# Gated cross-attention, one core: block transposes on VectorE in the setup, mp's rows placed by DMA, and the order of W1's loads

## Chip, cores and metric

The kernel runs on one core of a Trainium2 chip. The metric is device time of one execution in microseconds (us); lower is better. Everything is float32.

## What is computed

```python
memory_proj = einsum('bme,de->bmd', memory, W_mem)                 # mp
scores = einsum('bnd,bmd->bnm', x, memory_proj) / sqrt(D)
memory_context = einsum('bnm,bmd->bnd', softmax(scores), memory_proj)
gate = sigmoid(concat([x, memory_context], -1) @ W_gate.T + b_gate)
out = rmsnorm(x + gate * memory_context) * norm_w
```

There are 8 batches of 1024 rows of x (D = 1024), and for each batch 64 memory rows of 512 elements. W_gate has 1024 x 2048 elements. Its first half, here W1 (transposed), meets x. Its second half, W2, meets the memory context; since that context is a weighted sum of mp's rows, the kernel computes `mp @ W2 + b_gate` once, in the setup, and lets the attention weights sum its rows.

## The kernel before

**Setup.** All 512 memory rows (8 x 64, `BM`) are handled together, as 4 blocks of 128 rows (`NPAIR`).

1. Loads on SP's queue (`load`, L95-96) in this order: mem (4 transfers, L116-117), W_mem transposed as `wm` (4, L119-121), the bias, W2's first column half (16, L138), W1 into the tiles `ws1`, `ws7`, `ws3`, `ws2` (8 for each quarter, L143-148). W1 and W2 come in pieces of 32 partitions and 128 KB.
2. memT: 16 TensorE transposes into PSUM and 8 VectorE copies (L161-174). Four VectorE copies reorder wm into `wmp` (L176-184).
3. `pm`: 8 groups of 4 matmuls (the trace records two for each, so 64 in all) give mp transposed, chunk by chunk (L195-204). ScalarE and VectorE copy them in turn to the tiles `mpT`. After each second chunk ACT's queue stores the pair to `mpd` in HBM (`scratch`, L98-99).
4. mp's rows: 32 TensorE transposes of mpT into PSUM, 8 ScalarE copies, and 8 stores on ACT's queue to `mgd` (L206-221).
5. `pg`: 8 groups (n = 0 to 7, column half h by row block q) of 8 matmuls, again two records each, multiply mp by W2 (L400-425). VectorE adds the bias (`g2`, called g0 to g7 below by n), ACT stores it to `mgd` in two transfers. After group 0 the program issues the loads of W2's second half (`load_w2(1)`), of the first x tiles and of norm_w. After groups 0 to 5 VectorE gets its share of `w1_tasks`, the sums and differences of W1's quarters that the main loop multiplies by; after group 6 it gets `first`, the transposes and sums of the first x tiles.

**Main loop.** For each of 16 blocks of 512 rows, seven block products by a fast matrix multiplication scheme in two levels (`outer_product`, L533). Each has products kA, kB, kC, kD, kA, kE, kF in this order; VectorE and GpSimd combine them. x is transposed by VectorE in 32x32 blocks (`transpose_x`). The accumulators use five PSUM banks in rotation, the same that pm and pg use: kC of the very first product needs the bank that g7 still has to empty.

**What sets the order.** `pin` keeps the instructions of each engine in the order of the program. The framework puts the transfers of SP and ACT into an order of its own making and adds the waits between them. `gpool` has 7 buffers for W2 tiles, 4 for each half, so the fourth tile of the second half waits until group 3 has read the first tile of the first half. `mpT` takes the buffers of mem and of others, and the `mp` stages take wm's buffers (`xqpool`, 4), which the first x tiles take next.

```python
def inner_sums(o):
    w = ws[o]
    for s, a, b in ((T1, R12, R11), (T2, R22, T1), (R12, R22, R12), (T4, R21, T2)):
w1_tasks = [outer_sum(5, 7, 1), *inner_sums(1), outer_sum(6, 3, 5), outer_sum(7, 3, 7),
            outer_sum(4, 2, 6)] + [inner_sums of 6, 7, 5, 4, 2, 3]     # lambdas left out
```

Of the kernel before, what the change touches and what calls it, by code (L numbers as in the profile page):

```python
# [8 lines left out]
F32 = mybir.dt.float32  # L9
# [6 lines left out]
P = 128  # L16
# [4 lines left out]
def tile_gated_cross_attention_rmsnorm(  # L21
# [40 lines left out]
    nc = tc.nc  # L62
    B, N, D = x.shape
    M, E = mem.shape[1:]
# [3 lines left out]
    BM = B * M  # L68
    KD = D // P
    KE = E // P  # L70
    H = 512
    C = 256
    NPAIR = BM // P
    SCALE = 1.0 / float(D) ** 0.5
    Q4 = D // 4
# [3 lines left out]
    xqpool = ctx.enter_context(tc.tile_pool(name="xqpool", bufs=4))  # L79
    apool = ctx.enter_context(tc.tile_pool(name="apool", bufs=1))  # L80
    rot = ctx.enter_context(tc.tile_pool(name="rot", bufs=2))
# [3 lines left out]
    dram = ctx.enter_context(tc.tile_pool(name="dram", bufs=1, space=DRAM))  # L85

    pin = tc.keep_in_program_order

    def mm(o, lhsT, rhs, start, stop):
        pin(nc.tensor.matmul(o, lhsT, rhs, start=start, stop=stop, skip_group_check=True))  # L90

    def tt(eng, o, a, b, op):
        pin(eng.tensor_tensor(o, a, b, op))  # L93

    def load(o, i):  # L95
        pin(nc.sync.dma_start(o, i))

    def scratch(o, i):  # L98
        pin(nc.scalar.dma_start(o, i))

    def t4k(pool, shape, tag, name):
        return pool.tile(shape, F32, tag=tag, name=name)
# [7 lines left out]
    def bank(n, shape, name):  # L110
        return ps.tile(shape, F32, tag=banks[n % 5], name=name)


    memr = mem.rearrange("b m e -> (b m) e").rearrange("(q p) e -> p q e", p=P)
    mem_sb = [t4k(rot, [P, 2, E], "l2", f"mem_sb{i}") for i in range(2)]
    for q in range(NPAIR):  # L116
        load(mem_sb[q // 2][:, q % 2, :], memr[:, q, :])
    wm = []
    for k in range(KE):  # L119
        t = t4k(xqpool, [P, D], "xq", f"wm{k}")  # L120
        load(t, w_mem_t[k * P : (k + 1) * P, :])
        wm.append(t)
    bias_sb = t4k(small, [P, D], "junk", "bias_sb")
    load(bias_sb, b_gate.partition_broadcast(P))
    w2r = rows_by_chunk(w_gate_t[D:, :])
# [2 lines left out]
    def load_w2(h):  # L128
        for k in range(KD // 2):
            t = t4k(gpool, [P, 2, H], "gate", f"w2_{k}_{h}")  # L130
            for i in range(4):
                load(
                    t[32 * i : 32 * (i + 1), :, :],
                    w2r[i][:, 2 * k : 2 * k + 2, h * H : (h + 1) * H],
                )
            w2[k, h] = t
# [3 lines left out]
    w1r = rows_by_chunk(w_gate_t[:D, :])  # L140
    ws = {o: const.tile([P, 7, 2, C], F32, name=f"ws{o}") for o in range(1, 8)}
    R11, R21, R12, R22, T4, T1, T2 = range(7)
    for o, k, h in ((1, 0, 0), (7, 0, 1), (3, 1, 1), (2, 1, 0)):  # L143
        for i in range(4):
            for n in range(2):
                load(
                    ws[o][32 * i : 32 * (i + 1), 2 * n : 2 * n + 2, :, :],
                    w1r[i][:, 4 * k : 4 * k + 4, h * H + n * C : h * H + (n + 1) * C],
                )
    nw_sb = const.tile([P, D], F32, name="nw_sb")  # L150

    ident = const.tile([P, P], F32, name="ident")
# [3 lines left out]


    mpd = dram.tile([P, KD, BM], F32, name="mpd")
    mgd = dram.tile([B, 2, M, D], F32, name="mgd")
    memT = [t4k(apool, [P, 2, BM], f"a1{i + 1}", f"memT{i}") for i in range(2)]  # L160
    for q in range(NPAIR):  # L161
        pt = bank(q, [P, KE, P], f"pt_mem{q}")
        for k in range(KE):
            pin(
                nc.tensor.transpose(
                    pt[:, k, :], mem_sb[q // 2][:, q % 2, k * P : (k + 1) * P], ident
                )
            )
        for i in range(2):
            pin(  # L170
                nc.vector.tensor_copy(
                    memT[i][:, :, q * P : (q + 1) * P], pt[:, 2 * i : 2 * i + 2, :]
                )
            )
    wmp = []
    for k, tag in enumerate(("a21", "a22", "s1", "s2")):  # L176
        t = t4k(apool, [P, KD, P], tag, f"wmp{k}")
# [8 lines left out]
    mpT = [  # L186
        t4k(rot, [P, 2, BM], tag, f"mpT_{tag}_{i}")
        for tag in ("l2", "u")
        for i in range(2)
    ]  # L190

    def mp_rows(j, q):
        return mpT[j // 2][:, j % 2, q * P : (q + 1) * P]

    for j in range(KD):  # L195
        pm = bank(j, [P, BM], f"pm{j}")
        for k in range(KE):
            mm(pm, wmp[k][:, j, :], memT[k // 2][:, k % 2, :], k == 0, k == KE - 1)
        dst = mpT[j // 2][:, j % 2, :]
        if j % 2 == 0:  # L200
            pin(nc.scalar.copy(dst, pm))
        else:
            pin(nc.vector.tensor_copy(dst, pm))
            scratch(mpd[:, j - 1 : j + 1, :], mpT[j // 2])

    for q in range(NPAIR):  # L206
        stage = t4k(xqpool, [P, D], "xq", f"mp{q}")
        for h in range(2):
            pt = bank(2 * q + h, [P, 4, P], f"pt_mp{q}_{h}")
            for j in range(4):  # L210
                pin(nc.tensor.transpose(pt[:, j, :], mp_rows(4 * h + j, q), ident))
            pin(
                nc.scalar.copy(
                    stage.rearrange("p (i j r) -> p j i r", i=4, r=32)[
                        :, 4 * h : 4 * h + 4, :, :
                    ],
                    pt.rearrange("p j (i r) -> p j i r", r=32),
                )
            )
        for i in range(2):  # L220
            scratch(mgd[2 * q + i, 0], stage[i * M : (i + 1) * M, :])


    def outer_sum(o, a, b):
        tt(nc.vector, ws[o][:, 0:4, :, :], ws[a][:, 0:4, :, :], ws[b][:, 0:4, :, :], ALU.subtract)
# [4 lines that stand above are left out]
            yield lambda s=s, a=a, b=b: tt(  # L230
                nc.vector, w[:, s, :, :], w[:, a, :, :], w[:, b, :, :], ALU.subtract
            )
# [4 lines left out]
        *inner_sums(1),  # L237
        lambda: outer_sum(6, 3, 5),
        lambda: outer_sum(7, 3, 7),
        lambda: outer_sum(4, 2, 6),  # L240
    ] + [f for o in (6, 7, 5, 4, 2, 3) for f in inner_sums(o)]


    xq, A, S, L2, O = {}, {}, {}, {}, {}
    sTs, attns, attnTs, scs, mps, mgs = {}, {}, {}, {}, {}, {}
# [5 lines left out]
    def load_xq(q, t):  # L251
        b, n0 = where(q, t)
        xq[q, t] = tl = t4k(xqpool, [P, 4, Q4], "xq", f"xq{q}_{t}")
        src = x[b, n0 : n0 + P, :].rearrange("(s c) (i e) -> i c s e", c=32, i=4)
        for i in range(4):
            load(tl[32 * i : 32 * (i + 1), :, :], src[i])
# [47 lines left out]
    def inner_s(q, o, part):  # L304
        l11, l12, l21, l22 = quarters(left(q, o))
        if part == 0:
            L2[q, o] = t4k(rot, [P, 4, 2, P], "l2", f"l2_{q}_{o}")
        s1, s2, s3, s4 = (L2[q, o][:, i, :, :] for i in range(4))
        if part == 0:
            tt(nc.gpsimd, s1, l21, l22, ALU.add)  # L310
            tt(nc.gpsimd, s2, s1, l11, ALU.subtract)
        else:
            tt(nc.gpsimd, s3, l11, l21, ALU.subtract)
            tt(nc.gpsimd, s4, l12, s2, ALU.subtract)
# [71 lines left out]

    def load_mg(b):
        mgs[b] = t4k(small, [P, D], "mg", f"mg{b}")
        load(mgs[b], mgd[b].rearrange("g m d -> (g m) d"))


    first = [
# [7 lines left out]
    for h in range(2):  # L400
        cols = slice(h * H, (h + 1) * H)
        for q in range(NPAIR):
            pg = bank(n, [P, H], f"pg2_{h}_{q}")
            for k in range(KD):
                mm(pg, mp_rows(k, q), w2[k // 2, h][:, k % 2, :], k == 0, k == KD - 1)
            pool, tag = ((apool, "s4"), (small, "attnT"))[n % 2]
            stage = t4k(pool, [P, H], tag, f"g2_{h}_{q}")
            tt(nc.vector, stage, pg, bias_sb[:, cols], ALU.add)
            for i in range(2):
                scratch(mgd[2 * q + i, 1][:, cols], stage[i * M : (i + 1) * M, :])  # L410
            if n == 0:
                load_w2(1)
                for t in (0, 1, 2, 3):
                    load_xq(0, t)
                load(nw_sb, norm_w.partition_broadcast(P))
            if n < 6:
                while done < len(w1_tasks) * (n + 1) // 6:
                    w1_tasks[done]()
                    done += 1
            elif n == 6:  # L420
                for f in first:
                    f()
                for part in range(2):
                    inner_s(0, 1, part)
            n += 1
    load_mp(0)
    load_mg(0)


# [13 lines left out]
    def plan(q):  # L443
# [28 lines left out]
        if (q + 1) % QPB == 0:  # L472
            at(t0 + 10, load_mp, (q + 1) // QPB)
            at(t0 + 49, load_mg, (q + 1) // QPB)
# [219 lines left out]
```

## Time and profile before

| | |
|---|---|
| three runs | 1018.0, 1021.86, 1022.25 us; median 1021.86 us |
| the profiled execution | 1022.17 us, span 1020.4 us, mean granted TensorE clock 0.986 |
| TensorE / VectorE / ScalarE / GpSimd busy | 982.8 / 752.8 / 320.2 / 690.5 us |
| memT's transposes begin / pm begins | 3.32 / 9.03 us |
| transposes of mpT begin / pg begins | 39.59 / 46.71 us |
| first main product begins / its kC | 110.66 / 113.31 us |
| VectorE transpose of 128x512 (L267) | 693 ns mean |

Times inside the profile count from the start of the span. A row of the timeline tells start, duration, engine, line, operation, the tiles as out<-in, sizes, a count and, in brackets, how long the engine had been idle and what ended that. "SPq" and "ACTq" are the sequencers that issue transfers. In the tile names L93 and L90 are helper lines (`tt`, `mm`), so groups are told apart by tiles: ws and w are W1 and W2, g the stage of a pg group with its bias, l and s the sums made of x. A table by stages lists the stretch, its length, busy time and count for PE, PEld, DVE, ACT and POOL, and then granted clock, DMA share and GB/s. The chain of waits goes through the execution in order of time: start, duration, and what the end of the program was waiting for then.

### The profile page before, as it was taken

The page shows a single profiled execution, that of the slowest core. Times are in us where ns is not written, and L with a number is a line of the kernel's source. Part 1 is how long each engine was busy: PE and PEld are TensorE (multiplying, and loading weights), DVE is VectorE, ACT ScalarE, POOL GpSimd, SP SyncE. Part 2 cuts the span into 40 slices and gives each one's busy share as a digit, 9 for nine tenths or more (in the row PEclk, how much of TensorE's full clock was granted, in tenths as well). Part 3 has the DMA queues.
Part 4 walks back from the last instruction along what each step waited for, and adds up shares of the span by engine and source line. Part 5 has one row for each costly group of instructions (what it writes and reads, how often), then busy time and mean ns, then how long its engine had stood idle before and what let it go on. Part 6 is the DMA issues. An engine that isn't in the chain of part 4 may idle for free.

```text
span 1020.4 us, 14598 instructions
## 1 busy us (share of the span) xinstructions
PE 982.8 (96%) x4976; PEld 767.9 (75%) x4976; DVE 752.8 (74%) x1464; ACT 320.2 (31%) x587; POOL 690.5 (68%) x855
## 2 busy tenths in 40 slices
PE   7898999999999999999999999999999999999991
PEld 4443687888888887888788888888888878878881
DVE  2065667878878787878787787878787878878763
ACT  0200023334241523333243425142333334341512
POOL 0000477877878787878788787878787878878671
PEclk9899999999999999999999999999999999999996
DMA  7675608164643727192825455372718271543324
GB/s 246 185 187 152 169 1 171 68 140 108 153 106 83 186 76 162 63 187 83 166 73 132 117 131 128 81 188 69 170 62 184 86 165 70 125 128 83 84 72 134
DMA packets 75945, 126.78 MB, mean 124 GB/s; under 512 B 16224, under 2 KB 53088, under 8 KB 75872
## 3 DMA queue, kind: packets, MB, share of 16 engines
q1 hardware_dynamic: 64160, 86.01, 29.0%
q0 software_dynamic: 9216, 33.56, 17.9%
q10 hardware_dynamic: 2496, 6.29, 2.1%
q8 instruction: 39, 0.64, 0.3%
q14 instruction: 34, 0.28, 0.1%
HBM read 85.98 MB, written 39.85 MB: 123 GB/s over the span
## 4 chain that ended last, share of the span: by engine, by line
PE 82%; DVE 12%; DMA 3%; issue 1%; SPq 1%; ACT 0%; ACTq 0%; DVEq 0%; POOL 0%
PE kA L90 17%; PE pc L90 12%; PE kE L90 10%; PE kD L90 8%; PE kF L90 8%; PE kB L90 8%; PE kC L90 7%; PE psT L90 6%; DVE gate L518 5%; PE pm L90 3%; PE pg L90 3%; DVE gate L93 2%; DVE e L93 2%; DVE u L93 1%; DMA gate<-in_x 1%
## 5 line engine op out<-in xcount | busy, mean ns | idle before, releaser
L93 POOL TENSOR_TENSOR gate<-gate,u 128x256 f32<-128x256 f32 x336 | 269.1, 830 | 116.1 <-DVE u L93 92.8
L93 POOL TENSOR_TENSOR l<-a 128x256 f32<-128x256 f32 x128 | 125.5, 980 | 168.3 <-DVE a L267 104.8
L489 ACT ACTIVATE gate<-gate 128x512 f32<-128x512 f32 x128 | 79.3, 630 | 412.1 <-DVE gate L93 412.1
L90 PE MATMUL kA<-ws,a 128*128 128x256 f32 x512 | 131.5, 379 | 0.0
L90 PE MATMUL pc<-mg,attnT 64*128 64x256 f32 x512 | 127.4, 389 | 0.0
L518 DVE SCALAR_TENSOR_TENSOR gate<-gate,ss,nw_sb 128x512 f32<-128x512 f32 x128 | 121.6, 963 | 1.1
L90 PE MATMUL kC<-ws,l 128*128 128x256 f32 x448 | 115.1, 379 | 0.8 <-DVE g L93 0.8
L90 PE MATMUL kD<-ws,l 128*128 128x256 f32 x448 | 115.0, 379 | 0.0
L90 PE MATMUL kB<-ws,l 128*128 128x256 f32 x448 | 115.0, 379 | 0.0
L90 PE MATMUL kF<-ws,l 128*128 128x256 f32 x448 | 115.0, 379 | 0.0
L90 PEld LDWEIGHTS pc<-mg,attnT 64*128 64x128 f32 x512 | 90.6, 186 | 29.8 <-issue 21.2
L90 PEld LDWEIGHTS kA<-ws,a 128*128 128x128 f32 x512 | 97.2, 190 | 13.8 <-DVE s L93 0.2
L90 PE MATMUL kA<-ws,s 128*128 128x256 f32 x384 | 100.2, 383 | 0.0
L90 PEld LDWEIGHTS kB<-ws,l 128*128 128x128 f32 x448 | 85.1, 190 | 11.6
L90 PEld LDWEIGHTS kF<-ws,l 128*128 128x128 f32 x448 | 85.1, 190 | 11.6
L90 PEld LDWEIGHTS kC<-ws,l 128*128 128x128 f32 x448 | 83.8, 190 | 11.8 <-POOL l L93 1.1
L90 PEld LDWEIGHTS kD<-ws,l 128*128 128x128 f32 x448 | 83.9, 190 | 10.7
L93 DVE TENSOR_TENSOR gate<-gate,pc 128x512 f32<-128x512 f32 x128 | 87.1, 681 | 5.3 <-ACT gate L489 5.1
L267 DVE STREAM_TRANSPOSE a<-xq 128x512 f32<-128x512 f32 x128 | 86.0, 693 | 0.0
L93 POOL TENSOR_TENSOR l<-s 128x256 f32<-128x256 f32 x96 | 77.6, 809 | 8.4 <-PE kF L90 5.8
L90 PEld LDWEIGHTS kA<-ws,s 128*128 128x128 f32 x384 | 71.6, 190 | 15.2 <-DVE a L93 6.2
L93 DVE TENSOR_TENSOR u<-u,kB 128x256 f32<-128x256 f32 x112 | 46.8, 418 | 46.3 <-PE kB L90 41.6
(84 smaller groups left out, 1688.0 us busy)
## 6 DMA issues: line engine op xcount, KB each, us to landing
xq<-in_x SPq DMA_DIRECT2D x256, 128.0 KB, 5.5
gate<-in_x POOLq DMA_DIRECT2D x64, 512.0 KB, 7.4
out<-gate SPq DMA_DIRECT2D x64, 512.0 KB, 2.6
w<-in_w_gate_t SPq DMA_DIRECT2D x32, 128.0 KB, 3.3
ws<-in_w_gate_t SPq DMA_DIRECT2D x32, 128.0 KB, 2.9
mg<-mgd SPq DMA_DIRECT2D x8, 512.0 KB, 3.6
wm<-in_w_mem_t SPq DMA_DIRECT2D x4, 512.0 KB, 6.8
mgd<-mp ACTq DMA_DIRECT2D x8, 256.0 KB, 4.4
```

The source lines that it names most:

```text
L90: pin(nc.tensor.matmul(o, lhsT, rhs, start=start, stop=stop, skip_group_check=True))
L93: pin(eng.tensor_tensor(o, a, b, op))
L267: nc.vector.transpose(A[key][:, :, r * P : (r + 1) * P].rearrange("p j (s c) -> p s j c", c=32), xq[q, t].rearrange("p s (j r) -> p s j r" ...
L489: pin(nc.scalar.activation(g, g, AF.Sigmoid))
L518: nc.vector.scalar_tensor_tensor(g[:, cols], g[:, cols], rstd[:, t % 2 : t % 2 + 1], nw_sb[:, cols], ALU.mult, ALU.mult,)
```

## The change

The mem rows are loaded in 8 transfers of 32 partitions, in a layout from which four VectorE transposes in 32x32 blocks make memT without PSUM. For that wm's rows are loaded in another order, in 16 transfers of 32 partitions. mp's rows are made the same way: after each pair of pm chunks VectorE transposes four blocks of mpT into `mpq`, and after the last pair ACT issues 16 stores that put each 32-partition part in its place in `mgd`. The layout of `mgd` changes, so that a bias result is one store instead of two, and the load of mg is two instead of one. The last quarter of W1 (`ws2`) is loaded after W2's second half, and `outer_sum(4, 2, 6)`, which needs it, stands later in `w1_tasks`.

```diff
+    memq = [t4k(rot, [P, BM // 64, E // 4], "l2", f"memq{i}") for i in range(2)]
+    memr = mem.rearrange("b m e -> (b m) e").rearrange(
+        "(g s c) (i e) -> g i c s e", g=2, c=32, i=4
+    )
+    wm = [t4k(xqpool, [P, D], "xq", f"wm{k}") for k in range(KE)]
+    wmr = w_mem_t.rearrange("(i j r) d -> i j r d", i=4, r=32)
+    for g in range(2):
+        for i in range(4):
+            load(memq[g][32 * i : 32 * (i + 1), :, :], memr[g, i])
     for k in range(KE):
-        t = t4k(xqpool, [P, D], "xq", f"wm{k}")
-        load(t, w_mem_t[k * P : (k + 1) * P, :])
-        wm.append(t)
+        for i in range(4):
+            load(wm[k][32 * i : 32 * (i + 1), :], wmr[i, k])
...
-    for o, k, h in ((1, 0, 0), (7, 0, 1), (3, 1, 1), (2, 1, 0)):
+    def load_w1(o, k, h):
         for i in range(4):
             for n in range(2):
                 load(ws[o][...], w1r[i][...])
+    load_w1(1, 0, 0)
+    load_w1(7, 0, 1)
+    load_w1(3, 1, 1)
...
-    mgd = dram.tile([B, 2, M, D], F32, name="mgd")
+    mgd = dram.tile([2, BM, D], F32, name="mgd")
...
-    (16 TensorE transposes and 8 VectorE copies)
+    for g in range(2):
         for i in range(2):
             pin(
+                nc.vector.transpose(
+                    memT[i][:, :, g * (BM // 2) : (g + 1) * (BM // 2)].rearrange(
+                        "p j (s c) -> p s j c", c=32
+                    ),
+                    memq[g].rearrange("p s (j r) -> p s j r", r=32)[:, :, 2 * i : 2 * i + 2, :],
                 )
             )
...
+    mpq = [t4k(xqpool, [P, 4, Q4], "xq", f"mpq{g}") for g in range(4)]
     for j in range(KD):
...
+            pin(nc.vector.tensor_copy(src[:, 1, :], pm))
+            scratch(mpd[:, j - 1 : j + 1, :], src)
+            for g in range(4):
+                pin(
+                    nc.vector.transpose(
+                        mpq[g].rearrange("p s (j r) -> p s j r", r=32)[:, :, j - 1 : j + 1, :],
+                        src[:, :, g * P : (g + 1) * P].rearrange("p j (s c) -> p s j c", c=32),
+                    )
                 )
-    (32 TensorE transposes, 8 ScalarE copies, 8 stores to mgd)
+    for g in range(4):
+        for i in range(4):
+            scratch(
+                mgd[0, g * P : (g + 1) * P, i * Q4 : (i + 1) * Q4].rearrange(
+                    "(s c) e -> c s e", c=32
+                ),
+                mpq[g][32 * i : 32 * (i + 1), :, :],
+            )
...
         lambda: outer_sum(7, 3, 7),
+        *(f for o in (7, 5) for f in inner_sums(o)),
         lambda: outer_sum(4, 2, 6),
-    ] + [f for o in (6, 7, 5, 4, 2, 3) for f in inner_sums(o)]
+        *(f for o in (6, 4, 2, 3) for f in inner_sums(o)),
...
         mgs[b] = t4k(small, [P, D], "mg", f"mg{b}")
-        load(mgs[b], mgd[b].rearrange("g m d -> (g m) d"))
+        for g in range(2):
+            load(mgs[b][g * M : (g + 1) * M, :], mgd[g, b * M : (b + 1) * M, :])
...
-            for i in range(2):
-                scratch(mgd[2 * q + i, 1][:, cols], stage[i * M : (i + 1) * M, :])
+            scratch(mgd[1, q * P : (q + 1) * P, cols], stage)
             if n == 0:
                 load_w2(1)
+                load_w1(2, 1, 0)
                 for t in (0, 1, 2, 3):
                     load_xq(0, t)
```

More of the change, by code (lines that the diff above doesn't have):

```diff
@@ L111, in bank @@
         return ps.tile(shape, F32, tag=banks[n % 5], name=name)
[L114 to L118, printed above, removed]
+    memq = [t4k(rot, [P, BM // 64, E // 4], "l2", f"memq{i}") for i in range(2)]
[7 more added lines that the diff above has]
+            load(memq[g][32 * i : 32 * (i + 1), :, :], memr[g, i])
     for k in range(KE):
-        t = t4k(xqpool, [P, D], "xq", f"wm{k}")
-        load(t, w_mem_t[k * P : (k + 1) * P, :])
-        wm.append(t)
+        for i in range(4):
+            load(wm[k][32 * i : 32 * (i + 1), :], wmr[i, k])
     bias_sb = t4k(small, [P, D], "junk", "bias_sb")
@@ L158, in tile_gated_cross_attention_rmsnorm @@
     mpd = dram.tile([P, KD, BM], F32, name="mpd")
-    mgd = dram.tile([B, 2, M, D], F32, name="mgd")
+    mgd = dram.tile([2, BM, D], F32, name="mgd")
     memT = [t4k(apool, [P, 2, BM], f"a1{i + 1}", f"memT{i}") for i in range(2)]
[L161 to L168, printed above, removed]
+    for g in range(2):
         for i in range(2):
             pin(
-                nc.vector.tensor_copy(
-                    memT[i][:, :, q * P : (q + 1) * P], pt[:, 2 * i : 2 * i + 2, :]
+                nc.vector.transpose(
[3 more added lines that the diff above has]
+                    memq[g].rearrange("p s (j r) -> p s j r", r=32)[:, :, 2 * i : 2 * i + 2, :],
                 )
@@ L198, in tile_gated_cross_attention_rmsnorm @@
             mm(pm, wmp[k][:, j, :], memT[k // 2][:, k % 2, :], k == 0, k == KE - 1)
-        dst = mpT[j // 2][:, j % 2, :]
+        src = mpT[j // 2]
         if j % 2 == 0:
-            pin(nc.scalar.copy(dst, pm))
+            pin(nc.scalar.copy(src[:, 0, :], pm))
         else:
[L203 to L217, printed above, removed]
-                )
-            )
-        for i in range(2):
-            scratch(mgd[2 * q + i, 0], stage[i * M : (i + 1) * M, :])
+            pin(nc.vector.tensor_copy(src[:, 1, :], pm))
[6 more added lines that the diff above has]
+                    )
+                )
+    for g in range(4):
[5 more added lines that the diff above has]
+                mpq[g][32 * i : 32 * (i + 1), :, :],
+            )
     def outer_sum(o, a, b):
@@ L239, in tile_gated_cross_attention_rmsnorm @@
         lambda: outer_sum(7, 3, 7),
+        *(f for o in (7, 5) for f in inner_sums(o)),
         lambda: outer_sum(4, 2, 6),
-    ] + [f for o in (6, 7, 5, 4, 2, 3) for f in inner_sums(o)]
+        *(f for o in (6, 4, 2, 3) for f in inner_sums(o)),
+    ]
     xq, A, S, L2, O = {}, {}, {}, {}, {}
@@ L408, in tile_gated_cross_attention_rmsnorm @@
             tt(nc.vector, stage, pg, bias_sb[:, cols], ALU.add)
-            for i in range(2):
-                scratch(mgd[2 * q + i, 1][:, cols], stage[i * M : (i + 1) * M, :])
+            scratch(mgd[1, q * P : (q + 1) * P, cols], stage)
             if n == 0:
                 load_w2(1)
+                load_w1(2, 1, 0)
                 for t in (0, 1, 2, 3):
```

## The prediction

> **What bounds the kernel now.** I read the page's busy shares first, then the table by stages, then the chain of waits in the first 110 us, then the rows of SP and VectorE in it.
>
> ```profile
> PE 982.8 (96%) x4976; PEld 767.9 (75%) x4976; DVE 752.8 (74%) x1464; ACT 320.2 (31%) x587; POOL 690.5 (68%) x855
> ```
> TensorE bounds the whole, and its idle time lies at the start. By stages (PE busy first, granted clock third from last):
>
> ```profile
> 9.00:39.60 30.60, 30.57 (x65) 13.27 (x66) 4.16 (x6) 2.34 (x4) 0.00 (x0) 1.00 0.65 198
> 39.60:46.71 7.11, 4.08 (x33) 3.37 (x32) 0.69 (x1) 3.23 (x6) 0.00 (x0) 0.94 0.68 195
> 77.21:89.93 12.72, 8.94 (x17) 3.32 (x16) 6.06 (x10) 0.00 (x0) 0.00 (x0) 0.88 0.76 197
> 400.00:600.00 200.00, 199.15 (x1064) 163.37 (x1064) 162.90 (x326) 70.69 (x129) 157.49 (x195) 1.00 0.44 114
> ```
> The main loop has no slack to give; the change doesn't touch it. What it can move is when that loop starts: its third product, kC, at 113.31 us. The chain of waits shows what leads there:
>
> ```profile
> 9.03 30.73 PE pm L90 x64
> ...
> 64.40 2.28 DMA mgd<-g
> 66.68 0.02 issue
> 66.70 0.31 SPq L96
> ...
> 68.48 3.10 DMA ws<-in_w_gate_t
> ...
> 80.24 2.66 DMA mgd<-g
> 82.90 0.02 issue
> 82.92 0.31 SPq L96
> ```
> A load of W1 on SP starts when a store of ACT has landed, though the two share no data. The rows of SP fit one rule: SP's and ACT's transfers stand in one common order, and each waits for the landing of the one eight places ahead (the fourth piece of W2 starts at 8.19, when the first wm, eight ahead, has landed). In all, to 115 us:
>
> ```profile
> SPq L96 <- DMA mgd<-g: 29.2, 8, 5.1
> SPq L96 <- DMA mpd<-mpT_u: 10.2, 1, 10.2
> SPq L96 <- DMA mpd<-mpT_l: 9.7, 2, 5.1
> ```
> So weights arrive at the pace of TensorE's own results, and late weights stop TensorE and VectorE:
>
> ```profile
> 82.28 1.98 PE L90 MATMUL pg<-w,mpT_u 128*128 128x512 f32 x4 [1.47 <-DMA w<-in_w_gate_t]
> 86.58 3.56 PE L90 MATMUL pg<-w,mpT_u 128*128 128x512 f32 x4 [2.31 <-DMA w<-in_w_gate_t]
> 113.31 1.10 PE L90 MATMUL kC<-ws,l 128*128 128x256 f32 x4 [0.75 <-DVE g L93]
> ```
>
> **The skill.** "DMA: Bandwidth & Descriptors", Rules for kernel authors, says that transfers to separate partition parts serialize and that one of 128 partitions should be used. The trace agrees in part: four wm of 512 KB land 1.27 us apart (8.17 to 11.98), while 128 KB pieces of 32 partitions land 0.57 to 0.60 us apart, 2.3 us for 512 KB. "TensorE: Matmul & The Clock Gate", Part 1, says that TensorE runs at half speed after idling until it has been busy some 3.4 us. Here matmuls come every 0.85 us until 15.1 and every 0.43 us after, and again 0.85 from 46.71 to 52.8. "VectorE: DVE Perf Modes", The three transpose paths, says that VectorE transposes within 32x32 blocks only; the kernel's own x transposes do so in 0.69 us per 128x512.
>
> **Step 1, loads of mem and wm: later by 4.3 us.** Eight transfers become 24 of 128 KB. The first should land at 3.2 (issue at 0.74, plus the 2.5 us from issue to landing of unhindered pieces), the rest 0.57 apart: mem complete at 7.2, the last wm at 3.2 + 23 x 0.57 = 16.3 instead of 11.98. Bounds: the issue pitch of 0.47 gives 14.0, the 0.61 at which x pieces land gives 17.2. mem's rows of 512 B are shorter than any load's here but mpb's 256 B; at 18 ns per 256 B packet and 46 ns per 1 KB, 256 packets on 16 engines need about 0.45 us, less than the pitch. memT's 16 TensorE transposes and 8 copies become 4 transposes of 128x512, 0.69 each: two after 7.2 give 8.6, before the first wm (9.5): nothing on the path. If mem came 1 us later this cover would be gone, and every microsecond beyond would count.
>
> **Step 2, pm: ends at 43.5 instead of 39.6.** Copy of the last wm, 0.69: 17.0. The last pair of pm0 at half speed: 18.8. Seven more groups of 8 at 0.43: 24.0, to 42.8; some matmuls still slow, 0 to 1.7, taken as 0.7.
>
> **Step 3, transposes of mp leave TensorE.** The stage from 39.6 to 46.71 (7.1 us) goes, and with it the slow restart: the first eight pg matmuls took 6.5 us (46.71 to 53.18), the others 3.43; 3.0 more. In its place VectorE makes 16 transposes of 128x256, about 0.4 each from half of 0.69, four per pair of pm groups of 6.9 us: covered (their tiles take wm's buffers, free at 17.0); only the last four (1.6 us) delay the stores. pg group n then ends at 43.5 + 6.87(n+1), all eight at 98.5 if W2 comes in time, instead of 110.66. W2's first half (landed by 26.8 before) has 16 more transfers ahead of it: about 30, still covered by pm.
>
> **Step 4, the stores and SP's waits.** Now what was hidden: at 43.5 some 17 of 24 W1 pieces (before: 24 of 32), 16 of W2 and the moved 8 are still to come. The pair mpT store lands about 47.3. Then 16 stores of mp rows go through ACT instead of 8, from 44.7. At 0.5 us an issue (0.45 and 0.6 alternate in ACT's rows) they end at 53; with the loads among them, at the 0.44 us per 128 KB that both together reached there (300 GB/s), the first bias result g0 behind them in ACT's queue lands at 57 (60.4 before). That releases the last W1 pieces of the third quarter, landing at 60.5. VectorE then does two outer sums (2.25 each) and three inner (0.63): g2 at 66.9, landed at 70.2 (78.2 before, because g2 stood behind the outer sum that needs the fourth quarter). About 15 loads wait for that: the last of W2, then the moved quarter. It lands at 70.2 + 15 x 0.57 + 2.5 = **81.2**; W2's last at 76.7, where TensorE wants it at 76.1: a stall of 0.6 instead of 5.9. One store per bias result instead of two, and two mg loads instead of one, are off the path (mg is first used 27 us into the loop).
>
> **Step 5, what is late next: VectorE behind the moved quarter.** Behind outer_sum(4) in VectorE's order stand g3 to g7, 16 inner sums and the first transposes. From the rows of before: outer 2.25; four times g, 0.61; inner 16 x 0.63 = 10.0; the first x transposes, two sums and g7, 104.61 to 113.17, 8.6. Sum 23.3, so kC starts at 81.2 + 23.4 = 104.6 instead of 113.31: **8.7 us earlier**. TensorE, done with pg, kA and kB at 100.8, waits 3.8 us and may turn slow again: 0 to 3.0 us, by what the pause before 46.71 cost; I take 1.2. GpSimd's first sums follow the first two transposes, as before, and are done under the rest of them. On SP the moved 8 transfers pass W2's 16 and now stand before the 16 x pieces, nw, mpb and mg: 8 x 0.57 = 4.6 us later for all of them, if nothing else held them. x pieces now wait for g3 to g6; by the same rule the last lands about 98, when its transpose is due: no more than 2 us.
>
> **Sum.** +4.3 -0.4 (pm) -10.1 (transposes and slow restart) -5.3 (W2 stall) = -11.5 on TensorE's side, which the wait for VectorE cuts to -8.7, and the slow clock to -7.5. The profiled execution took 1022.17 (span 1020.4), giving 1014.7; the median of the runs is 0.3 lower: 1014.5.
>
> **Rivals.**
> TensorE-bound: the common order is kinder, the quarter lands by 77, and pg's end at 98.5 decides; kC at about 101, 12 us earlier: 1010. For it: loads alone, unhindered, would land by then. Against it: 29 us of SP's waits in before were for g.
> No change: g2 or g0 lands some 5 us later, the quarter at 86 to 88, kC at 109 to 111, less up to 3 for the clock: 1020.5. For it: a different place of the stores in the common order, which the profile of before can't show.
> Slower: the sixteen stores on ACT. Before, ACT issued its eight in 42.08 to 50.5, 1.05 us each, copies included. If the 16 go at 1.4, held by landings eight places ahead, they end at 67.4, g0 lands at 70, the quarter at 94.2, kC at 117.6, 4.3 later, with 1 for the clock: 1027.5. It decides from about 1.15 us per store, where the quarter lands at 90 and kC is at its old place. Against it: the copies that spaced them are gone.
> That the change does not do what it says: the PE transposes certainly go, so this leaves only their time returned elsewhere, as above.
>
> **Chances.** Forecast (1012 to 1017) 0.47; TensorE-bound 0.15; no change 0.25; slower 0.13. So faster by over 0.5% (5.1 us, about what a measurement of this kernel can tell) 0.62, within 0.25, slower 0.13. The range runs from the TensorE-bound case with no slow clock, 1009, to the upper end of no change, 1022; the slower rival stays outside.
>
> **What would show it.** The last wm landing near 16.3 and pm ending at 43.5; no gap between pm and pg, at 0.43 us a matmul; g0, g2 and the moved quarter landing near 57, 70 and 81; TensorE waiting for VectorE's g ahead of kC, near 104.6; the main loop unchanged. I am wrong if the stores take over 1 us each, if SP still waits over 20 us for g, or if the loop itself changes pace.

## The result, and the profile after

| | before | after | ratio, 95% interval |
|---|---|---|---|
| 6 runs each | 1019.04 us (1017.26 to 1022.25) | 1018.95 us (1016.15 to 1019.72) | 0.999 [0.9967, 1.0013] |
| later: after in 21 runs, before in 50 | 1019.39 us | 1016.84 us | 0.9977 [0.9966, 0.9988] |
| the profiled executions | 1022.17, span 1020.4 us | 1017.62, span 1015.5 us | |

The first six runs can't be told from no change; the later ones show a gain of 0.2%, small but clear of its interval. The forecast was 1014.5 us, 0.7% under before. Its range (1009 to 1022) held the time, but it is wide enough to hold the rival "no change" too, and by the gain that rival is the case that came: both medians of after, 2 us apart, lie within 0.5% of before. In two runs below, the repeat of before and the first with all setup stores on GpSimd, single executions were disturbed (1.7 to 2.2 times as long); they are left out of the times given, and so are those runs' profiles.

The busy row first: TensorE has 48 instructions and 11 us less, and is the bound as before.

```profile
PE 971.7 (96%) x4928; PEld 759.7 (75%) x4928; DVE 757.7 (75%) x1476; ACT 316.2 (31%) x579; POOL 691.2 (68%) x855
```

The table by stages of after, for most of pm, the pg groups up to the end of their stall, the slow restart after it, and the last stretch ahead of kC (stretch, length, busy time and count of PE, PEld, DVE, ACT, POOL, then clock, DMA share, GB/s):

```profile
18.00:44.00 26.00, 25.50 (x60) 11.32 (x60) 7.10 (x17) 2.34 (x4) 0.00 (x0) 1.00 0.61 178
44.00:79.00 35.00, 32.35 (x76) 14.06 (x74) 18.15 (x23) 0.00 (x0) 0.00 (x0) 1.00 0.78 221
79.00:83.00 4.00, 3.43 (x5) 1.64 (x6) 0.00 (x0) 0.00 (x0) 0.00 (x0) 0.57 0.85 216
104.00:108.30 4.30, 1.37 (x8) 0.89 (x6) 4.11 (x5) 0.00 (x0) 1.65 (x3) 1.00 0.74 164
```

ACT's engine is idle in the last three of these stages (its eight copies of mp's rows are gone), and between 104 and kC VectorE is busy nearly all the time while TensorE is not. The matmul rows of after give the same in time:

```profile
43.57 3.60 PE L90 MATMUL pg<-w,mpT_l 128*128 128x512 f32 x8
...
79.57 3.46 PE L90 MATMUL pg<-w,mpT_u 128*128 128x512 f32 x4 [3.21 <-DMA w<-in_w_gate_t]
...
108.29 1.10 PE L90 MATMUL kC<-ws,l 128*128 128x256 f32 x4 [2.93 <-DVE g L93]
```

pg follows pm with no gap and at full clock. One stall for W2 is left, and at kC TensorE waits 2.9 us for VectorE's g7. kC is at 108.29 instead of 113.31, 5.0 us earlier; from kC to the end of the span it is 907.2 us, 907.1 before. The main loop is untouched, and the whole difference between the profiles lies ahead of kC. What led there is in the chain of waits of after:

```profile
18.58 25.17 PE pm L90 x58
...
46.50 5.48 DMA mgd<-mpq
...
59.45 2.05 DMA mgd<-mpq
61.51 0.31 SPq L96
61.87 4.68 DMA ws<-in_w_gate_t
66.67 4.50 DVE ws L93 x2
...
73.85 2.06 DMA mgd<-g
75.93 0.31 SPq L96
...
84.70 2.29 DVE ws L93
...
108.29 1.10 PE kC L90 x4
```

Stores of mp's rows release loads of W1, those release sums, a bias result's store releases SP again, and behind that comes the moved quarter (its last piece lands at 84.57), whose outer sum starts at 84.70, 23.6 us ahead of kC. (The view puts that sum's wait down to a piece of x, which landed only at 85.14; the quarter is what it reads.) The chain is the one that the prediction drew, some 3.4 us late at its end. The sums of SP's waits to 115 us (what it waited for: us in total, times, longest):

```profile
SPq L96 <- DMA mgd<-g: 22.4, 7, 5.4
...
SPq L96 <- DMA mpd<-mpT_l: 8.8, 2, 4.9
SPq L96 <- DMA mgd<-mpq: 5.8, 1, 5.8
SPq L96 <- DMA mpd<-mpT_u: 5.1, 1, 5.1
```

The waits for bias results fell from 29.2 to 22.4 us, and those for stores of mp's rows rose from 2.7 to 5.8. One more thing can be read from the traces: the landings of SP's and ACT's transfers are told by the same eight semaphores, which both queues use in turn. That is the common order of the prediction, in which each transfer waits for the one eight places ahead.

### The profile page after: what moved, and what is told of

It reads as the page before. It is cut to its first block, busy times and chain, and to the rows that moved or that the text cites. A ratio compares the mean times of both kernels' runs of the same rounds, so it can differ in the third digit from the quotient of the medians.

```text
span 1015.5 us, 14542 instructions
## 1 busy us (share of the span) xinstructions
PE 971.7 (96%) x4928; PEld 759.7 (75%) x4928; DVE 757.7 (75%) x1476; ACT 316.2 (31%) x579; POOL 691.2 (68%) x855
## 4 chain that ended last, share of the span: by engine, by line
PE 79%; DVE 13%; DMA 5%; issue 1%; SPq 1%; ACT 0%; DVEq 0%; ACTq 0%; POOL 0%
PE kA L90 17%; PE pc L90 12%; PE kE L90 10%; PE kD L90 8%; PE kF L90 8%; PE kB L90 8%; PE kC L90 7%; PE psT L90 6%; DVE gate L526 5%; PE pm L90 2%; DVE gate L93 2%; DVE e L93 2%; DMA mgd<-mpq 1%; DVE ws L93 1%; DVE u L93 1%
## 5 line engine op out<-in xcount | busy, mean ns | idle before, releaser
L93 DVE TENSOR_TENSOR u<-u,kB 128x256 f32<-128x256 f32 x112 | 46.7, 417 | 44.9 <-PE kB L90 41.6
```

## Why the two profiles differ by more than the medians

The first theory: the profile before was an unlucky execution, and part of the gain was only ever there against it. The rival: before is usually like its profile, and after loses something that its own profile doesn't show. Before was therefore run again, unchanged, with its medians taken from many runs, and profiled once more.

> The kernel before once more, unchanged. Theory A (the change saves 5 us of setup in every execution, and something outside the setup varies by as much): kC starts near 113.3 us again and the rest of the span takes 907 us give or take the variation. Theory B (the profiled execution of before was a bad one, its setup itself varies): kC starts clearly earlier than 113, near 108 to 110, and the span is about 1015.5.

Measured: 1019.6 us (12 runs), ratio 1.0002 [0.9987, 1.0017] to before on the same chip. The second profile:

> The kernel before once more, for its profile. If its setup varies with where TensorE's slow stretches fall: the granted clock's slow stretches lie elsewhere than in the first profile (slow until 15.1, 45.8 to 52.6, 86.8 to 90.2), kC moves by multiples of about 1.7 us from 113.3, and the span moves with it. If not: kC at 113.3 within 0.5.

Measured: 1022.49 us, kC at 113.90, so again an execution at the top of before's runs (1016.3 to 1023.2 over all of them, medians of the batches 1019.2 to 1019.8). These two profiles differ by 0.6 us at kC and show the same slow stretches of TensorE's clock. The profiled before, in two stages:

```profile
46.00:53.00 7.00, 6.29 (x8) 2.69 (x9) 0.00 (x0) 1.73 (x4) 0.00 (x0) 0.53 0.93 279
86.00:91.00 5.00, 4.42 (x7) 1.90 (x8) 0.83 (x2) 0.00 (x0) 0.00 (x0) 0.66 0.88 208
```

After the transposes of mp the clock is near a half for 6.8 us, and after the W2 stall again for 3.4. Does every execution of before pay that? Its runs, sorted by mean granted clock: at 0.986, 25 runs with a median of 1022.4 us; at 0.987, 33 with 1019.8; at 0.989, 20 with 1017.1. So executions of the same kernel differ by 5 us with 0.3% of clock, and both profiles of before are of its 0.986 kind. The profile of after is of the 0.989 kind. At 0.989 and above, before has 1017.1 us (42 runs) and after 1016.5 (14 of its later 21): at equal clock under 1 us is left. That figure is rough, since after's times hardly go with its clock (1016.8 us in its seven runs below 0.989). The first theory stands: the profiles of before are some 3 us above its usual run. Which stretches the better runs lack was not seen, since no run of before with a clock of 0.989 was profiled.

## The experiments on the parts

**One part each.** Theory: the new order of W1 brings what gain there is, and the transposes on VectorE give back on the load side what they save on TensorE. Rival: the transposes' removal is the gain, and the order only lets it through. First after again, beside them:

> The changed kernel once more. Theory A: kC near 108.3 again, ratio to before about 0.995. Theory B: kC near 108.3 and a ratio of 0.999 to 1.000, with the kernel before on the same chip starting its loop at about the same time.

Measured: 1016.84 us, 0.9977 [0.9966, 0.9988]; kC at 106.26, wm's last at 16.71, g0 landed at 61.62, the quarter at 82.64. Everything on the load side is 1 to 2 us earlier than in the first profile of after, while the span after kC is 1.3 us longer (a slow stretch of the clock begins at kC).

Only the order (before, with the last quarter of W1 behind W2's second half and its outer sum after the inner sums of 7 and 5):

```diff
-    for o, k, h in ((1, 0, 0), (7, 0, 1), (3, 1, 1), (2, 1, 0)):
+    for o, k, h in ((1, 0, 0), (7, 0, 1), (3, 1, 1)):
...
                 load_w2(1)
+                load_w1(2, 1, 0)
```

> The kernel before with only the last quarter of W1 moved behind W2's second half (and outer_sum(4, 2, 6) later); transposes stay on TensorE. If the order of loads is what gains: TensorE's wait for W2 in pg group 4 falls from 5.9 to under 3 us, the quarter lands at 80 to 85 us, kC at 104 to 109, some 5 us earlier than in the kernel before. If the transposes are what gains: kC stays at 112 to 113.

Measured: 1012.97 us (1012.54 to 1013.38), 0.9929 [0.991, 0.9948]. Only the transposes (after, with the quarter and the sums in their old order):

```diff
     load_w1(3, 1, 1)
+    load_w1(2, 1, 0)
...
                 load_w2(1)
-                load_w1(2, 1, 0)
```

> The changed kernel with the last quarter of W1 back in its old place and the old order of sums. If the order of loads is what gains: with eight more loads ahead of W2 TensorE waits 7 to 9 us in pg group 4, and kC comes at 111 to 114, no gain over the kernel before although 7 us of TensorE transposes are gone. If the transposes are what gains: kC at 106 to 108.

Measured: 1018.99 us, 0.9998 [0.9987, 1.0009]. The order alone gains 0.7%, the transposes alone nothing, and the two together less than the order alone. Part of the order's 6.4 us goes with the clock: its six runs all have 0.990 or 0.991, and against before's runs at 0.989 and above it gains 4.2. Its profile has no stall for W2 and no slow stretch there. The chain of only the order:

```profile
4.02 7.55 DMA wm<-in_w_mem_t
...
12.34 25.17 PE pm L90 x58
...
43.32 1.08 ACT mp L218 x2
...
44.45 15.71 PE pg L90 x32
...
60.90 2.28 DMA mgd<-g
...
75.64 3.98 DMA ws<-in_w_gate_t
79.80 2.29 DVE ws L93
...
103.82 1.10 PE kC L90 x4
```

It has TensorE's transposes of mp still, and they stand in the chain: pm ends at 37.5, ACT copies and stores mp's rows, pg begins at 44.45. Yet its g0 lands at 57.15 and its quarter at 79.62, 6 and 5 us before after's (4.5 and 3 us before the repeat's). Then come the same 24 us to kC. So TensorE's 7 us are less than what after loses elsewhere: its pm ends 6.2 us later, and sixteen stores stand ahead of its g0. (Against before, pm ends 2.2 us earlier here, since the clock rose earlier in this execution; whether that is chance was not shown.) The rows of only the transposes show where their saving goes:

```profile
72.38 5.37 PE L90 MATMUL pg<-w,mpT_l 128*128 128x512 f32 x8 [2.35 <-DMA w<-in_w_gate_t]
...
79.66 1.96 PE L90 MATMUL pg<-w,mpT_u 128*128 128x512 f32 x4 [1.91 <-DMA w<-in_w_gate_t]
84.10 1.98 PE L90 MATMUL pg<-w,mpT_u 128*128 128x512 f32 x4 [2.48 <-DMA w<-in_w_gate_t]
```

pg starts at 42.4 instead of 46.7, but waits 6.7 us for W2 where before it waited 3.8: its last W2 piece lands at 84.06 (86.44 before), because W1's last quarter is ahead of it. Its kC is at 109.17, between the two expectations, and 4.1 us ahead of the profiled before, which is near the top of that kernel's runs; in the medians nothing is left.

**The sixteen stores.** Theory: they cost ACT 15 us and delay g0, and with it SP. Rival: what delays SP is where pm's own stores land. Four stores of 512 KB instead (mp's rows in HBM in an order that a whole `mpq` tile can be written to, each mg in two loads from there and one for the bias half):

```diff
-    for g in range(4):
-        for i in range(4):
-            scratch(mgd[0, ...], mpq[g][32 * i : 32 * (i + 1), :, :])
+    for g in range(4):
+        scratch(mp4[g], mpq[g])
```

> The changed kernel with mp's rows stored by four transfers of 128 partitions and 512 KB, in the layout of mpq, instead of sixteen; the load of mg puts the parts in place (three transfers instead of two). If the sixteen stores in the common order with SP's loads are what the transposes cost: g0, behind 4 stores instead of 16, lands by 55 instead of 63, g2 near 70 instead of 76, the moved quarter near 78 instead of 85, kC near 102 to 103, some 6 us earlier than in the changed kernel. If the later start of pm (24 small loads) is what costs: kC stays within 1 us of 108.3.

Measured: 1017.27 us, 0.9968 [0.9957, 0.998]. The stores are issued by 48.45 instead of 60.25, g0 lands at 53.68 instead of 63.17, and the quarter lands at 83.12, hardly earlier (84.57, 82.64), with kC at 106.71 (108.29, 106.26). Nine microseconds gained at g0 became 1.5 at most. The waits of SP in this run:

```profile
SPq L96 <- DMA mgd<-g: 25.0, 7, 4.8
SPq L96 <- DMA mp<-mpq: 9.6, 3, 8.8
SPq L96 <- DMA mpd<-mpT_l: 8.8, 2, 5.0
SPq L96 <- DMA mpd<-mpT_u: 5.1, 1, 5.1
```

SP waits 8.8 us at one go for a store of mp's rows. The loads of W1 still stand in a common order with stores that pm paces, and then with bias results that pg paces. The stores' number is not the cause: after and this kernel are the same within their intervals.

**The small loads.** Theory: wm in 16 pieces starts pm late, and all that pm paces comes late with it. Rival: the transposes on VectorE delay something themselves. For this, mp's rows by VectorE with the four stores and the new order, but mem, memT and wm as before:

> Only the later part of the change, with four stores: mem and wm are loaded as in the kernel before (8 transfers) and memT comes from TensorE; mp's rows come from VectorE with four stores of 512 KB; W1's last quarter is moved. If the later start of pm costs on its own: pm ends near 37.5 to 39.5, pg begins at once, and kC comes 3 to 6 us before that of the four-store kernel, near 97 to 99. If the loads' order after pm alone decides: kC within 1.5 us of the four-store kernel.

Measured: 1011.51 us, 0.9924 [0.9904, 0.9944]. And the same with nothing changed but wm in 16 pieces of 32 partitions:

```diff
-        load(t, w_mem_t[k * P : (k + 1) * P, :])
+        for i in range(4):
+            load(t[32 * i : 32 * (i + 1), :], w_mem_t[k * P + 32 * i : k * P + 32 * (i + 1), :])
```

> The kernel mix (mem and memT as in the kernel before, mp's rows from VectorE with four stores, W1's last quarter moved) with only wm loaded in 16 pieces of 32 partitions instead of 4 of 128. If the small pieces are what delays pm and with it all that follows: the last wm lands near 15 instead of 12, pm ends 2 to 3 us later, SP's stream follows it, and the kernel is 2.5 to 4 us slower than mix (ratio to before about 0.9955). If the late start is taken up by later waits: within 1 us of mix (0.9924).

Measured: 1017.24 us, 0.9981 [0.9969, 0.9994]. So wm's cut alone costs 0.57%, more than four_stores (the same as mix but for mem, memT and wm) loses against mix, 0.44%. Rows of mix, then of mix with wm in 16:

```profile
9.79 29.51 PE L90 MATMUL pm<-memT,wmp 128*128 128x512 f32 x64 [1.86 <-DVE wmp L186]
...
39.14 3.60 PE L90 MATMUL pg<-w,mpT_l 128*128 128x512 f32 x8
...
100.76 1.22 PE L90 MATMUL kC<-ws,l 128*128 128x256 f32 x4 [4.41 <-DVE g L93]
```

```profile
16.05 26.01 PE L90 MATMUL pm<-memT,wmp 128*128 128x512 f32 x58 [0.26 <-DVE wmp L187]
...
105.67 2.04 PE L90 MATMUL kC<-ws,l 128*128 128x256 f32 x4 [5.18 <-DVE g L93]
```

The last wm lands at 15.18 instead of 13.37, pm ends at 42.06 instead of 39.30, the quarter lands at 80.92 instead of 77.17, and kC is 4.9 us later. A start 1.8 us later grew to 4.9 on the way: some of it is pm's clock (at half from 10.97 to 17.80, in mix only until 12.86), some a wait of the sums for an x piece (1.8 us). Mix and only the order are equal within their intervals (0.9924, 0.9929): mp's rows by VectorE, well placed, gain nothing that the times can show. On the way from pg to kC most of the saving is lost: pg begins 5.3 us earlier than in only the order, the quarter lands 2.5 earlier, kC comes 3.1 earlier, and a slow stretch at kC takes 1.4 of that back in the profiled execution. In mix TensorE waits 4.4 us at kC for VectorE, which waits for the quarter.

**The common order.** Theory: SP's loads come late because their transfers share an order with ACT's stores. Rival: the 16 DMA engines are full there, and another order changes nothing. All setup stores were moved to GpSimd's queue:

```diff
     def scratch(dst, src):
-        pin(nc.scalar.dma_start(out=dst, in_=src))
+        pin(nc.gpsimd.dma_start(out=dst, in_=src))
```

In after:

> The changed kernel with all stores of the setup issued from GpSimd's queue instead of ACT's. If SP waits because its loads share one order with ACT's stores: SP's waits for g and mpq vanish, loads land every 0.55 to 0.6 us without a break, W2 is complete before TensorE wants it at 76, the moved quarter lands before 75, and kC is set by TensorE and g6, near 101 to 102. If the DMA engines or the bytes are the limit: the loads land as late as in the changed kernel, quarter near 84, kC near 108.

Measured: 1009.7 us (five runs), 0.9909 [0.9888, 0.993]. Once more, for a profile:

> The changed kernel with stores on GpSimd's queue once more, for a profile at full clock: no waits of SP for stores, W2 complete before 76 us, no wait in pg, kC near 101 to 102.

Measured: 1009.58 us, kC at 100.29, pg from 42.81 to 97.90 without a break, the quarter at 75.16, although g0 lands at 60.58, only 1 us earlier than in the repeat of after. GpSimd's stores use eight landing semaphores of their own. The chain from the end of pm to kC is now TensorE's work almost alone:

```profile
42.97 54.93 PE pg L90 x128
```

In before:

> The kernel before, only with the setup's stores on GpSimd's queue. If the common order of loads and stores is the limit of the setup before: W2 lands in time, the wait of 5.9 us in pg group 4 goes, kC comes 6 to 7 us earlier, ratio about 0.993. If the order of the loads themselves (W1's last quarter ahead of W2) is the limit: TensorE still waits for W2, ratio above 0.997.

Measured: 1009.17 us, 0.9898 [0.9875, 0.992], kC at 101.47. SP's longest waits there:

```profile
SPq L96 <- PE pg L90: 12.8, 1, 12.8
SPq L96 <- DVE a L267: 11.1, 2, 10.6
...
SPq L96 <- DMA mgd<-g: 6.5, 1, 6.5
```

It now waits for W2's buffer, which pg has to free, and for x's, with W1 already there (its last quarter at 47.39, 71.58 before). The theory stands, and after is the clean case of it: the same bytes come early enough once loads do not wait for stores. In before a second effect is mixed in. ACT no longer issues stores between its copies of mp's rows, so these run in one go, and pg begins at 43.88 instead of 46.71, at full clock:

```profile
40.60 4.20 ACT L213 COPY mp<-pt_mp 128x512 f32<-128x512 f32 x8 [3.29 <-PE pt_mp L211]
```

With the stores on GpSimd's queue, before and after stand at 1009.2 and 1009.7: the whole change is then worth nothing.

**The best version.** Mix with the stores on GpSimd's queue:

> The kernel mix with the setup's stores on GpSimd's queue. If both causes (small loads ahead of pm, one order for SP's loads and ACT's stores) are right and separate: SP never waits for a store, pm ends near 38, pg has no wait for W2, kC is set by TensorE and the g chain, near 96 to 98, about 4 us before the same step in the changed kernel with stores on GpSimd: some 1006 us, ratio 0.987. If a bound that I have not seen remains (x pieces, VectorE's sums): ratio about 0.991 as with the changed kernel.

Measured: 1005.51 us (1004.91 to 1006.67), 0.9867 [0.9845, 0.9889], 1.3% under before. Its rows:

```profile
38.99 3.60 PE L90 MATMUL pg<-w,mpT_l 128*128 128x512 f32 x8
...
90.49 3.60 PE L90 MATMUL pg<-w,mpT_u 128*128 128x512 f32 x8
...
96.48 1.10 PE L90 MATMUL kC<-ws,l 128*128 128x256 f32 x4 [0.67 <-DVE g L93]
```

From 9.5 us on TensorE only pauses 0.7 us ahead of kC. Here the transposes' removal does count: pg starts 4.9 us earlier than in before with GpSimd's stores, and kC is 5.0 earlier; pg runs without a break in both. Of the 4.9 us, 1.0 is pm's earlier end and the rest TensorE's stage, which is down to 3.75 us there (40.13 to 43.88). By the medians the gain is 3.7 us, with pm's early start kept by the large loads. The saving is worth something only where TensorE is what comes last.

## Where the prediction was right and where it was wrong, step by step

That the time fell into the range is partly luck: a gain of 0.7% was forecast and 0.1 to 0.2% came, and two terms of the sum failed, its base and Step 4.

**The base of the sum failed.** The working took the profiled execution (1022.17 us) and three runs' median (1021.86) for the kernel's time, and counted the slow restart of 3.0 us at pg as a fixed cost that the change takes away. Before's median over many runs is 1019.4; its restart and the second slow stretch depend on the execution. "The Trainium skill", page "TensorE: Matmul & The Clock Gate", Part 1, says that the window is free-running and that the number of slow matmuls varies from run to run. The runs agree: in the setup slow stretches last 3.41 us or twice that, and before's runs spread over 7 us. After the same pause of 2.14 us ahead of pg, TensorE was slow for 6.83 us in both profiles of before and for 3.41 in only the order. So about 2.5 us of the 7.5 were no gain over the usual run.

**Step 1** (loads of mem and wm 4.3 us later) was right in kind and 0.4 to 1.4 us short: the last wm landed at 17.71 (16.71 in the repeat) against 16.3, with about the expected pitch (0.55 to 0.56, 0.57 expected), but mem was complete at 8.74 instead of 7.2 (7.80 in the repeat).

**Step 2** (pm ends at 43.5) came out right, 43.74 and 42.74, but two errors cancel in it: in the first profile pm began its long run 1.6 us late (18.58 instead of 17.0), and then had none of the slow matmuls for which some 1.6 us had been allowed. What it missed is what hangs on pm's end. The stores of mpT that pm paces landed at 26.81, 33.47, 40.29 and 50.17, where only the order has 21.17, 27.22, 34.33 and 40.93, and SP's loads wait for them.

**Step 3** (TensorE's stage of 7.1 us and the restart go) was right as a statement on TensorE, pg beginning with no gap, and wrong as a term of the sum: the order alone, with that stage in place, is faster than after.

**Step 4** is the second that failed. The stores went at 0.95 us each (45.05 to 60.25), not at 0.5:

```profile
45.05 15.21 ACTq L99 DMA_DIRECT2D mgd<-mpq  x16
60.35 1.14 ACTq L99 DMA_DIRECT2D mgd<-g  x2
```

The fourth of them waited from 48.28 to 50.19 for the last store of mpT, eight places ahead, which landed at 50.17 where Step 4 had put it at 47.3. g0, ready at 51.3, reached ACT's sequencer at 60.35 and landed at 63.2 instead of 57; the third quarter's last piece landed at 66.6 instead of 60.5, g2 at 75.9 instead of 70.2, the moved quarter at 84.6 instead of 81.2, and TensorE's stall was 3.2 us instead of 0.6. (The 5.9 us that the working gives for before's stall are 3.8 of waiting; the rest is mostly the slow clock after it.) This is the mechanism of the rival "slower", at two thirds of its 1.4 us. But four_stores shows that making the stores few does not bring those 3.4 us back; the loads go on waiting for whatever store stands eight ahead. With g0 at 53.7, earlier than predicted, the third quarter's last piece still landed at 62.7 instead of 60.5 there. The lateness came from the common order as a whole, not from ACT's rate alone; with the stores on GpSimd's queue, and after otherwise as it is, the quarter lands at 75.16.

**Step 5** (23.4 us from the quarter to kC) was right: 23.7 in after, 23.6 to 24.2 in the other runs in which the quarter decides, save 24.75 in mix_wm16. TensorE waited 2.9 us there (3.8 predicted); the slow clock, taken at 1.2 us, cost nothing in the first profile of after and some 1.7 us in the repeat, at kC and kD.

**The sum** against its own base: kC is 5.0 us earlier instead of 8.7. The 3.4 us of Step 4 and 0.3 of the chain make the difference; the 1.2 us for the slow clock did not come. Against the usual run of before the base takes some 2.5 of the 5.0. Of the prediction's signs of error, the one on SP came true (over 20 us waited for bias results: 22.4). The time fits the rival "no change", and its mechanism is near too, with the quarter at 84.6 where it said 86 to 88 and kC at 108.3 where it said 109 to 111.

By parts, in ratios to before, each on top of the one ahead of it: the order -0.7%; mp's rows by VectorE with four stores -0.05%, within the intervals; the small loads of mem and wm, with memT by VectorE, +0.44% (four_stores over mix); sixteen stores instead of four +0.09%, within the intervals. These are steps from before to after, so they add up to after's 0.9977 by themselves; in another sequence a part can be worth something else, as mix with GpSimd's stores shows.

What stays open: why the first six runs of after stood 2 us above its later 21, and in which stretches a good run of before differs from its profiles. GpSimd's queue was only tried for all stores of the setup together, and the removal of the waits was not tried with the stores left on ACT.

## What to carry over

Before costing a saved stage, find which wait ends last behind it: here most of TensorE's 7 us were lost in loads that waited for stores, and cutting the first loads into small pieces cost more than the stage was worth. When two queues share an order of transfers, a load's time is set by the stores it stands behind, so try another queue for the stores before trimming them. And take the base from many runs: a single profile can sit 3 us above the kernel's usual time, more than many changes are worth.

## What was not expected of the hardware

- The page "DMA: Bandwidth & Descriptors" of the Trainium skill, in Rules for kernel authors, says that spreading transfers over issuing engines does not help bandwidth and saves only issue time. Here moving the setup's stores to GpSimd's queue took 1.0% off before (part of it by freeing ACT between its copies) and 0.6% off the mix (0.9924 to 0.9867). That doesn't contradict the page, which speaks of bandwidth: the waits between SP's loads and the stores went.
- 0.3% of mean clock goes with 0.5% of time between executions of one kernel: 1022.4 us at 0.986, 1017.1 at 0.989.
- Stores of 128 KB, 16 in a row on ACT's queue among loads of SP, went out 0.95 us apart; with GpSimd issuing them in after, 0.75 (44.76 to 56.69, 16 stores). Both figures hold one wait for the last store of mpT, 1.9 and 2.9 us.
- Short pauses can bring the slow clock, and longer ones need not: in the repeat of after a pause of 2.38 us ahead of kC brought a slow stretch of 3.41 us, in the first profile one of 2.93 us at the same place brought none.
